# A four-layer graph network on one core: comparing adjacency counts four to a word, moving one PSUM tile and one matrix product, and one store to another queue

## The chip, the cores and the metric

The kernel runs on one core of a Trainium2 chip. The metric is the device time of a launch in microseconds, the median of the runs. A core has TensorE (PE) for matrix products and transposes, VectorE (DVE), ScalarE (ACT) and GpSimd (POOL) for the rest, and SyncE (SP), which here issues most of the DMA transfers; each of them works through its own queue of instructions, and they wait for one another by semaphores. The engines work on SBUF (128 partitions) and on PSUM, the banks that PE writes its products to.

## The reference, cut to what matters

A graph has 6250 nodes of 64 features and 206,250 directed edges: 100,000 edges in both directions, and a loop at every node. So the matrix A of edge counts between nodes is symmetric. Four layers follow one another, each on the normalised and clipped node features, each added to them:

```python
x = x + _L0_gnn_ref(h, ...)   # two graph convolutions: sums over the edges, with norm
x = x + _L1_gnn_ref(h, ...)   # one such sum
x = x + _L2_gnn_ref(h, edge_attr_64, src, dst, ...)
x = x + _L3_gnn_ref(edge_index, h)   # three such sums
```

The sums of layers L0, L1 and L3 are products of A (with norms) and the features. L2 alone uses the edges' own features:

```python
Vp = leaky_relu(V @ pAw + pAb) @ pBw + pBb
x = relu(E @ mlp_w1 + mlp_b1)
x = relu(x @ mlp_w2 + mlp_b2)
scale = sigmoid(x @ Bw + Bb)
shift = x @ Cw + Cb
msg = scale * Vp[src] + shift
M = clip(msg, EPS, None) ** 2
ssum = segment_sum(M, dst, n)          # and the root of its mean
```

## The kernel before

**Nodes and A.** The nodes make 49 blocks of 128 (`NB`), seven chunks (`NC`) of seven blocks (`CB`, 896 nodes, `W`). The first stage, up to about 535 us, counts the edges by products of one-hot matrices (PE L903, evicted by ACT L907) into a strip of half a chunk's columns, 14 strips (`CS`), and SP stores each finished strip to DRAM (L914) as FP8 counts in seven tensors `A[0]` to `A[6]`. The same stage computes the first convolution (PE L1042).

**Two sums, 535 to 1003 us.** `gather` (L1183) goes over A by 49 pieces of 896 x 896 counts (784 KB): SP loads a piece (L1187), PE makes 49 products with it (L1190), and 7 pieces make a chunk of sums. SP issues in the order of the program: the last strip's store, then the pieces.

**The edges, 1003 to 3654 us.** The edges come in 202 groups `G` of 1024 (8 to a partition, `J`). An order written out by hand for PE, ACT and DVE runs 208 slots (`slot`, L1588 on). Slot i works on several groups at once, in this order of code:

- `loaded(i+4)`: SP loads edge features `e` (L1500).
- `evicted` h2 of group i-3: ACT, from PSUM bank `p_2` (L1522).
- `biased`, `gated` of i-4: DVE adds the bias to the gates and shifts in `p_bc` (L1533), ACT takes the sigmoid (L1538).
- `read_them`: a comparison or an addition left from the slot before.
- `clipped` of i-4: DVE multiplies by the fetched `v` (L1543), adds the shift (L1544), clips (L1545).
- `fetched(i)`: POOL issues eight indirect gathers of `Vp` rows (L1506) into one of four buffers `v`; `turned_edges(i)`: PE transposes `e` (L1514); `layer` 1 of i-1 (L1518).
- half of the slot's work beside (see below).
- `squared`, `compared_nodes` of i-4: ACT squares the message twice (L1552 to bf16, L1553 to PSUM `p_m`, which is a buffer of the ring `p_sum`), DVE makes one-hot matrices `to` (L1558) and takes the rest that bf16 lost (L1612, L1624; ACT L1613).
- `added_to_nodes` of i-6 (DVE L1575 to L1583).
- `layer` 2 of i-2 into `p_2` (PE L1518), then `gates_and_shifts` of i-3 into `p_bc` (PE L1528); `p_bc` and `p_2` have one buffer each.
- evictions on ACT of `p_e` and `p_1`; the last part of the message on DVE (L1624).
- the other half of the work beside; `summed` of i-5 (PE L1566).

**Work beside.** The list `todo` is spread over the slots up to a chunk's end, n items a slot. It has three kinds of item:

- `here` loads a piece of A on SP.
- `crossed` is the check that A is symmetric. For 28 pairs of chunks (i, k) it turns a block of the piece on PE by products with the identity (L1412), three or four blocks to a PSUM tile of the ring `p_sum` (two buffers), and DVE compares it with the piece `there` from the other side of A (L1418), adding up the differences into one column of `unlike`. A pair has 14 such items, all 392. `there` is loaded on SP by one transfer a pair (L1405).
- `partial` is a part of L3's first sum: 21 products on PE (L750) into the ring `p_sum`, which DVE adds to `Y` (L1437).

The first four pairs of chunks are checked alone, in the first 35 or so slots; after that each chunk of nodes that is finished brings 56 comparisons, 14 sums and 7 loads over about 29 slots. At the end the differences are added up; if there are any, a general path computes everything without relying on the symmetry.

**The end, 3723 to 4127 us.** Two more passes of `gather` over A make the rest of L3.

Of the kernel before, what the change touches and what calls it, by code (L numbers as in the profile page):

```python
# [617 lines left out]
def fast(ctx, tc, bad, x, src, dst, edge_attr, W3, b3, W4, b4, w1, b1, w2, b2, Bw, Bb, Cw, Cb,  # L618
# [10 lines left out]
    def strip_of(s, bs):  # L629

        lo, hi = OF_CHUNK[s % 2]
        return A[s // 2][:, bs, lo * P:hi * P]
# [40 lines left out]
    def blocks(c):  # L673
        return slice(c * CB, (c + 1) * CB)
# [83 lines left out]
    def first_stage(ph):  # L758
# [136 lines left out]
        def placed(s, q, n, lo, hd):  # L895

            if q == 0:
                strips[s] = new_strip()
            for r in range(2 * n):
                p = psum.tile([P, SG, P], F32, name="p_a", bufs=2)  # L900
                for j in range(SG):
                    g = r * SG + j
                    nc.tensor.matmul(p[:, j, :2 * NB], lo[:, g // GQ, :, g % GQ],  # L903
                                     hd[:, g // GQ, :, g % GQ], start=True, stop=True)
                col = 2 * (q * 2 + r) * SG

                nc.scalar.activation(  # L907
                    strips[s][:, :, col:col + 2 * SG].rearrange("p b (j l) -> p b j l", l=2),
                    p[:, :, :2 * NB].rearrange("p j (b l) -> p b j l", l=2), AF.Copy,
                    saturate=False)  # L910
                if r % 2:
                    if q + n == portions(s) and r == 2 * n - 1:
                        lo_, hi_ = OF_CHUNK[s % 2]
                        nc.sync.dma_start(strip_of(s, slice(0, NB)),  # L914
                                          strips[s][:, :, :(hi_ - lo_) * P])
                    yield

        waiting = []
# [447 lines left out]
    with ExitStack() as ph:  # L1366
# [12 lines left out]
                 ((2, 6), (2, 3), (2, 4), (2, 2)), ((3, 6), (3, 4), (3, 5), (3, 0)),  # L1379
                 ((4, 6), (4, 5), (4, 0), (4, 1)), ((5, 6), (5, 0), (5, 1), (5, 2)))  # L1380
        FIRST = ((3, 3), (4, 4), (5, 5), (6, 6))
        unlike = cpool.tile([P, 28 * 2 * CB], F32, name="unlike")

        def order(pairs):
            ks = [k for _, k in pairs]
# [14 lines left out]
        def there(n):  # L1400

            if n < len(there_of):
                i, k = there_of[n]
                t = held["there", i, k] = mpool.tile([P, CB, W], COUNT, name="there", bufs=2)
                nc.sync.dma_start(t, A[i][:, blocks(k), :])  # L1405

        def crossed(n, i, k, b, a0, a1):
            if b == 0 and a0 == 0:
                there(there_of.index((i, k)) + 1)
            p = ps_a.tile([P, 4, P], F32, name="p_sum", bufs=2)  # L1410
            for a in range(a0, a1):
                nc.tensor.matmul(p[:, a - a0, :], held["here", i, k][:, a, b * P:(b + 1) * P], ident_b,  # L1412
                                 start=True, stop=True)
            of_there = held["there", i, k][:, b, a0 * P:a1 * P]

            def compared():
                junk = mpool.tile([P, 4 * P], BF16, name="junk", bufs=1)
                nc.vector.scalar_tensor_tensor(  # L1418
                    junk[:, :(a1 - a0) * P],
                    p[:, :a1 - a0, :].rearrange("p a q -> p (a q)"), 15.5, of_there, op0=OP.min,  # L1420
                    op1=OP.not_equal, accum_out=unlike[:, n:n + 1])

            return compared

# [18 lines left out]
        def plan(pairs, sums):  # L1443
            for at, (i, k) in enumerate(order(pairs) if sums else pairs):
                asked.append((i, k))
                todo.append((here, len(asked)))
                if at < len(pairs):
                    for b in range(CB):
                        for a0, a1 in ((0, 4), (4, CB)):
                            todo.append((crossed, len(crossings), i, k, b, a0, a1))  # L1450
                            crossings.append((i, k, b, a0))
                if sums:
                    todo.append((partial, i, 2 * k))
                    todo.append((partial, i, 2 * k + 1))
# [65 lines left out]
        def evicted(g, p, t, **how):  # L1520
            of[g][t] = mpool.tile([P, 512], F32, name=t)
            nc.scalar.activation(of[g][t], of[g].pop(p), **how)  # L1522
# [13 lines left out]
        def gated(g):  # L1536
            gate = of[g]["p_bc"][:, :, 0, :]
            nc.scalar.activation(gate, gate, AF.Sigmoid)  # L1538
# [8 lines left out]
        def squared(g):  # L1547
            m = of[g].pop("m")
            m3 = of[g]["m3"] = mpool.tile([P, J, 3, D], BF16, name="m3")
            p_m = of[g]["p_m"] = ps_a.tile([P, 512], F32, name="p_sum", bufs=2).rearrange(  # L1550
                "p (j f) -> p j f", f=D)
            nc.scalar.activation(m3[:, :, 0, :], m, AF.Square)  # L1552
            nc.scalar.activation(p_m, m, AF.Square)  # L1553
# [33 lines left out]
        def slot(i):  # L1587
            def at(later):  # L1588
                return 0 <= i - later < G

            if i + 4 < G:
                loaded(i + 4)
            if at(3):
                evicted(i - 3, "p_2", "h2", func=AF.Relu, bias=b2_c)
            if at(M_AT):
                biased(i - M_AT)
                gated(i - M_AT)
            read_them()
            if at(M_AT):
                clipped(i - M_AT)  # L1600
            if at(0):
                fetched(i)
                turned_edges(i)
            if at(1):
                layer(i - 1, w1_d, "eT", "p_1")
            n = -(-len(todo) // max(min(k for k in ends if k >= i) + 1 - i, 1))
            some_of(n - n // 2)
            if at(M_AT):
                squared(i - M_AT)
                compared_nodes(i - M_AT)  # L1610
                p_m, m3 = of[i - M_AT].pop("p_m"), of[i - M_AT]["m3"]
                nc.vector.tensor_sub(p_m, p_m, m3[:, :, 0, :])  # L1612
                nc.scalar.activation(m3[:, :, 1, :], p_m, AF.Copy)  # L1613
            done = added_to_nodes(i - ADD_AT) if at(ADD_AT) else []
            if at(2):
                layer(i - 2, w2_d, "h1", "p_2")
            if at(BC_AT):
                gates_and_shifts(i - BC_AT)
            if at(0):
                evicted(i, "p_e", "eT", func=AF.Copy)  # L1620
            if at(1):
                evicted(i - 1, "p_1", "h1", func=AF.Relu, bias=b1_c)
            if at(M_AT):
                nc.vector.tensor_sub(m3[:, :, 2, :], p_m, m3[:, :, 1, :])  # L1624
            read_them()
            some_of(n // 2)
            if at(SUM_AT):
                summed(i - SUM_AT)
            for c in done:
                finished(c)  # L1630

# [4 lines left out]
                slot(i)  # L1636
            read_them()

        assert not todo and len(crossings) == 28 * 2 * CB


        nc.vector.tensor_reduce(missed[:, 2:3], unlike, axis=AX.X, op=OP.add)
        ones_c = cpool.tile([P, P], F32, name="ones_c")
        nc.vector.memset(ones_c, 1.0)
        p_m = ps_a.tile([P, 512], F32, name="p_e")
# [98 lines left out]
```

## Time and profile before

| what | value |
|---|---|
| runs | 4137.59, 4135.94, 4144.2 us; median 4137.59 |
| the profiled execution | 4129.13 us, its span 4127.2 us |
| granted TensorE clock, mean | 0.848 |
| PE, DVE, ACT, POOL busy, share of the span | 71%, 56%, 30%, 39% |
| DMA | 388.84 MB, mean 94 GB/s |
| 510 to 550 us: PE busy | 29.8 of 40 us |
| 550 to 1003 us: PE busy | 430 of 453 us |
| 1040 to 3620 us: PE, DVE, ACT, POOL busy | 1587, 1541, 823, 1512 of 2580 us |
| 3730 to 4127 us: PE busy | 389 of 397 us |

The profile is of one execution. Each row of its groups names a line of the kernel, the engine, the operation and its operands (out<-in), then the count, the busy time in all with the mean of one in ns, and the idle time that the engine had just before these instructions, with what ended it. "issue" is time in which the engine waited for nothing that the profile shows; "remote" or "another core or an unknown queue" is a wait whose end the profile can't place, since this is one core. PEld is PE's loading of weights, which overlaps its products. A name with q behind it (SPq) is the engine's queue of instructions that are not counted as work, such as the issue of a DMA.

### The profile page before, as it was taken

What the parts mean: (1) busy time and instruction counts of PE and PEld (TensorE: products, weight loads), DVE (VectorE), ACT (ScalarE), POOL (GpSimd) and SP (SyncE); (2) the same over time, 40 slices, a digit from 0 to 9 for tenths busy, and PEclk for the clock granted to TensorE, in tenths of its full rate; (3) what the DMA queues carried; (4) which work ended last, traced back from release to release, by engine and by line L of the source; (5) the groups of instructions that cost most, each with busy time, mean ns of one, the idle gap of its engine ahead of it and who ended that gap; (6) DMA issues with size and microseconds to landing.
All of it is one profiled execution on the core that took longest, in us unless ns stands there. A gap on an engine that the chain in (4) does not pass through costs nothing.

```text
span 4127.2 us, 60291 instructions
## 1 busy us (share of the span) xinstructions
PE 2926.0 (71%) x23962; PEld 2233.0 (54%) x23962; DVE 2309.9 (56%) x5293; ACT 1240.5 (30%) x2061; POOL 1611.4 (39%) x1885
## 2 busy tenths in 40 slices
PE   1799989997455566666666666655666666679999
PEld 1788889996233333333433343333434343349999
DVE  5999935322555566655656565655655565662111
ACT  3677710001233333333333232333323333320000
POOL 5000010002556655555555565565555555510000
PEclk9899999998777777787877787777778787789999
DMA  3243375653222222222222222222222222126664
GB/s 114 58 111 87 96 222 188 200 185 118 57 57 58 58 56 57 58 78 54 75 54 63 72 58 71 61 57 57 79 56 63 63 65 63 44 98 190 202 205 157
DMA packets 229091, 388.84 MB, mean 94 GB/s; under 512 B 93482, under 2 KB 139482, under 8 KB 228543
## 3 DMA queue, kind: packets, MB, share of 16 engines
q1 hardware_dynamic: 170478, 322.28, 25.1%
q0 software_dynamic: 54816, 60.71, 7.3%
q8 instruction: 190, 3.11, 0.3%
q10 hardware_dynamic: 3504, 1.90, 0.2%
q14 instruction: 103, 0.84, 0.1%
HBM read 340.54 MB, written 44.21 MB: 93 GB/s over the span
## 4 chain that ended last, share of the span: by engine, by line
PE 38%; DVE 32%; another core or an unknown queue 15%; issue 7%; ACT 4%; DMA 2%; POOL 1%; DVEq 0%; ACTq 0%; SPq 0%; POOLq 0%
PE p_acc L1190 18%; DVE to L1558 5%; PE p_bc L1528 4%; PE p L1518 4%; PE p_sum L750 4%; DVE p_bc L1533 3%; DVE junk L1418 3%; DVE m L1543 3%; DVE hd L888 3%; DVE m L1544 3%; DVE lo L888 2%; DVE p_sum L1612 2%; PE p_s L1566 2%; ACT p_bc L1538 2%
## 5 line engine op out<-in xcount | busy, mean ns | idle before, releaser
L1506 POOL DMA_INDIRECT v<-Vp_dram,src_g x1616 | 1544.3, 956 | 1471.1 <-DVE m L1543 608.1
L1190 PE MATMUL p_acc<-U,piece 128*128 128x192 bf16 x9604 | 800.3, 246 | 11.5 <-DMA piece<-A 9.1
L1190 PEld LDWEIGHTS <-piece 128*128 128x128 fp8e4 x9604 | 795.4, 98 | 16.7 <-DMA piece<-A 9.3
L1528 PE MATMUL p_bc<-BC,h 128*128 128x256 f32 x1616 | 532.5, 480 | 310.6 <-DVE m L1544 265.1
L1528 PEld LDWEIGHTS p_bc<-BC,h 128*128 128x128 f32 x1616 | 379.8, 243 | 559.0 <-issue 424.7
L1412 PE MATMUL p_sum<-ident_b,piece 128*128 128x128 bf16 x1372 | 157.8, 248 | 501.5 <-issue 159.8
L1533 DVE TENSOR_TENSOR p_bc<-p_bc,bias 128x1024 f32<-128x1024 f32 x202 | 248.5, 1230 | 443.6 <-remote 355.3
L1412 PEld LDWEIGHTS <-piece 128*128 128x128 fp8e4 x1372 | 109.0, 110 | 694.8 <-issue 501.2
L1418 DVE SCALAR_TENSOR_TENSOR junk<-p_sum,there 128x512 bf16<-128x512 f32 (+1 forms) x392 | 242.1, 618 | 258.2 <-remote 142.5
L1518 PE MATMUL p<-h,w_d 128*128 128x512 f32 x404 | 276.2, 768 | 102.5 <-ACT h L1522 77.0
L1522 ACT ACTIVATE h<-p,b_c 128x512 f32<-128x512 f32 x404 | 264.3, 694 | 277.4 <-remote 143.5
L1201 DVE TENSOR_REDUCE zg<-p_acc 128x128 f32<-128x384 f32 x112 | 56.3, 507 | 514.4 <-PE p_acc L1190 513.9
L907 ACT ACTIVATE strip<-p_a 128x784 fp8e4<-128x784 f32 x392 | 301.5, 822 | 101.1 <-PE p_a L903 86.0
L750 PE MATMUL p_sum<-piece,U 128*64 128x448 fp8e4 x2058 | 259.9, 379 | 73.0 <-issue 33.3
L1558 DVE TENSOR_SCALAR to<-count,lane 128x128 bf16<-128x128 bf16 x1616 | 291.9, 264 | 0.0
L1552 ACT ACTIVATE m<-m 128x512 bf16<-128x512 f32 x202 | 127.6, 632 | 503.3 <-DVE m L1545 397.4
L1538 ACT ACTIVATE p_bc<-p_bc 128x512 f32<-128x512 f32 x202 | 117.6, 582 | 461.0 <-DVE p_bc L1533 387.5
L1518 PE MATMUL p<-eT,w_d 128*128 128x512 f32 x404 | 251.1, 708 | 5.2 <-issue 2.8
L750 PEld LDWEIGHTS <-U 128*64 128x64 bf16 x2058 | 126.5, 116 | 208.7 <-issue 119.8
L1566 PE MATMUL p_s<-m,to 128*128 128x192 bf16 x1616 | 215.9, 288 | 31.0 <-DVE H L1580 10.3
L1042 PE MATMUL p_sum<-U,strip 128*128 128x192 bf16 x2401 | 230.3, 248 | 0.0
L888 DVE TENSOR_TENSOR lo<-count,key 128x4096 bf16<-128x4096 bf16 (+1 forms) x103 | 225.1, 2185 | 0.0
(204 smaller groups left out, 3289.1 us busy)
## 6 DMA issues: line engine op xcount, KB each, us to landing
piece<-A SPq DMA_DIRECT2D x249, 784.0 KB
e<-in_edge_attr SPq DMA_DIRECT2D x202, 256.0 KB
v<-Vp_dram,src_g POOLq DMA_INDIRECT x1616
A<-strip SPq DMA_DIRECT2D x7, 3136.0 KB
there<-A SPq DMA_DIRECT2D x28, 784.0 KB
A<-strip SPq DMA_DIRECT2D x7, 2352.0 KB
pairs<-pair SPq DMA_DIRECT2D x1, 1616.0 KB
Vp_dram<-v SPq DMA_DIRECT2D x7, 224.0 KB
```

The costliest lines, as they stand in the source:

```text
L750: nc.tensor.matmul(p[half * D:(half + 1) * D, :w], U3[:, b, k, :], at_block, start=(i < 2), stop=(i >= 3 * n - 2))
L888: nc.vector.tensor_tensor(t, of.unsqueeze(1).to_broadcast(t.shape), key[:, k, at:at + n * 2 * SG].rearrange("p (h j) -> p h j", j=GQ) .uns ...
L907: nc.scalar.activation(strips[s][:, :, col:col + 2 * SG].rearrange("p b (j l) -> p b j l", l=2), p[:, :, :2 * NB].rearrange("p j (b l) -> ...
L1190: nc.tensor.matmul(p[d // 2][:, d % 2 * 3 * D:(d % 2 + 1) * 3 * D], t[:, b, d * P:(d + 1) * P], U3[:, k * CB + b, :, :].rearrange("p t f - ...
L1412: nc.tensor.matmul(p[:, a - a0, :], held["here", i, k][:, a, b * P:(b + 1) * P], ident_b, start=True, stop=True)
L1418: nc.vector.scalar_tensor_tensor(junk[:, :(a1 - a0) * P], p[:, :a1 - a0, :].rearrange("p a q -> p (a q)"), 15.5, of_there, op0=OP.min, op1 ...
L1506: nc.gpsimd.indirect_dma_start(out=v[:, j, :], out_offset=None, in_=Vp_dram[:, :], in_offset=bass.IndirectOffsetOnAxis(ap=src_g[:, g, j:j ...
L1518: nc.tensor.matmul(of[g][p], w, of[g].pop(x), start=True, stop=True)
L1528: nc.tensor.matmul(p_bc[:, 2 * q:2 * q + 2].rearrange("p j o f -> p (j o f)"), h2[:, q * P:(q + 1) * P], BC, start=True, stop=True)
L1533: nc.vector.tensor_tensor(p_bc, p_bc, bias.unsqueeze(1).to_broadcast([P, J, 2, D]), op=OP.add)
L1558: nc.vector.tensor_scalar(to[:, j, :], count, lane[:, g, j:j + 1], None, op0=OP.is_equal)
L1566: nc.tensor.matmul(p, to[:, j, :], m3[:, j].rearrange("p t f -> p (t f)"), start=(j == 0), stop=(j == J - 1))
```

## The change

Four things are edited.

1. The store of the last strip is issued on ACT's queue instead of SP's, and all strips are stored as pairs of counts (a bf16 view of the same bytes).
2. The check looks at counts as FP32 words of four. `there` has another layout: row 4x + j of a block lies in partition x (32 partitions to a block) at place j, so that four rows lie behind one another in a partition; a pair is loaded by seven transfers, one a block. `crossed` turns 128 or 96 word columns of three or four blocks by PE's FP32 transpose, which makes the four counts of a word four rows, and compares 2048 or 1536 counts at once, reading the PSUM tile as counts and `there` in steps of one row (896 bytes). A pair has 4 items instead of 14; all are 112 instead of 392.
3. `p_m`, the squared message in FP32, lies in the bank `p_2` instead of the ring `p_sum`.
4. `layer` 2 of group i-2 is made at the slot's end, behind `summed`, instead of ahead of the gates; h2's eviction on ACT comes behind `biased` and `gated` in the next slot instead of ahead of them.

```diff
@@ -911,8 +911,9 @@
                     if q + n == portions(s) and r == 2 * n - 1:
                         lo_, hi_ = OF_CHUNK[s % 2]
-                        nc.sync.dma_start(strip_of(s, slice(0, NB)),
-                                          strips[s][:, :, :(hi_ - lo_) * P])
+                        (nc.sync if s < CS - 1 else nc.scalar).dma_start(
+                            strip_of(s, slice(0, NB)).bitcast(BF16),
+                            strips[s][:, :, :(hi_ - lo_) * P].bitcast(BF16))
...
-        unlike = cpool.tile([P, 28 * 2 * CB], F32, name="unlike")
+        HALVES = ((0, 4), (4, CB))
+        unlike = cpool.tile([P, 28, 2, 2], F32, name="unlike")
+        nc.vector.memset(unlike, 0.0)
...
-                t = held["there", i, k] = mpool.tile([P, CB, W], COUNT, name="there", bufs=2)
-                nc.sync.dma_start(t, A[i][:, blocks(k), :])
-
-        def crossed(n, i, k, b, a0, a1):
-            if b == 0 and a0 == 0:
+                t = held["there", i, k] = mpool.tile([P, 2, 4, W], COUNT, name="there", bufs=2)
+                for d in range(CB):
+                    nc.sync.dma_start(
+                        t[d % 4 * 32:d % 4 * 32 + 32, d // 4],
+                        A[i][:, k * CB + d, :].rearrange("(x j) w -> x j w", j=4))
+
+        def crossed(n, i, k, h, a0, a1):
+            if h == 0 and a0 == 0:
                 there(there_of.index((i, k)) + 1)
+            x0, x1 = HALVES[h][0] * 32, HALVES[h][1] * 32
+            m = x1 - x0
             p = ps_a.tile([P, 4, P], F32, name="p_sum", bufs=2)
+            words = held["here", i, k].bitcast(F32)
             for a in range(a0, a1):
-                nc.tensor.matmul(p[:, a - a0, :], held["here", i, k][:, a, b * P:(b + 1) * P], ident_b,
-                                 start=True, stop=True)
-            of_there = held["there", i, k][:, b, a0 * P:a1 * P]
+                nc.tensor.transpose(p[:m, a - a0, :], words[:, a, x0:x1], ident)
+            of_there = held["there", i, k][:m, h, :, a0 * P:a1 * P]
 
             def compared():
-                junk = mpool.tile([P, 4 * P], BF16, name="junk", bufs=1)
+                junk = mpool.tile([P, 4, P, 4], BF16, name="junk", bufs=1)
                 nc.vector.scalar_tensor_tensor(
-                    junk[:, :(a1 - a0) * P],
-                    p[:, :a1 - a0, :].rearrange("p a q -> p (a q)"), 15.5, of_there, op0=OP.min,
-                    op1=OP.not_equal, accum_out=unlike[:, n:n + 1])
+                    junk[:m, :a1 - a0],
+                    p[:m, :a1 - a0, :].bitcast(COUNT).rearrange("p a (r j) -> p a r j", j=4),
+                    15.5, of_there.rearrange("p j (a r) -> p a r j", r=P), op0=OP.min,
+                    op1=OP.not_equal, accum_out=unlike[:m, n // 4, h, a0 // 4:a0 // 4 + 1])
...
-                    for b in range(CB):
-                        for a0, a1 in ((0, 4), (4, CB)):
-                            todo.append((crossed, len(crossings), i, k, b, a0, a1))
-                            crossings.append((i, k, b, a0))
+                    for h in range(2):
+                        for a0, a1 in HALVES:
+                            todo.append((crossed, len(crossings), i, k, h, a0, a1))
+                            crossings.append((i, k, h, a0))
...
-            p_m = of[g]["p_m"] = ps_a.tile([P, 512], F32, name="p_sum", bufs=2).rearrange(
+            p_m = of[g]["p_m"] = ps_a.tile([P, 512], F32, name="p_2").rearrange(
...
-            if at(3):
-                evicted(i - 3, "p_2", "h2", func=AF.Relu, bias=b2_c)
             if at(M_AT):
                 biased(i - M_AT)
                 gated(i - M_AT)
+            if at(3):
+                evicted(i - 3, "p_2", "h2", func=AF.Relu, bias=b2_c)
             read_them()
...
             done = added_to_nodes(i - ADD_AT) if at(ADD_AT) else []
-            if at(2):
-                layer(i - 2, w2_d, "h1", "p_2")
             if at(BC_AT):
                 gates_and_shifts(i - BC_AT)
...
                 summed(i - SUM_AT)
+            if at(2):
+                layer(i - 2, w2_d, "h1", "p_2")
```

The final addition over `unlike` follows its new shape.

More of the change, by code (lines that the diff above doesn't have):

```diff
@@ L1637, in fast @@
             read_them()
-        assert not todo and len(crossings) == 28 * 2 * CB
-        nc.vector.tensor_reduce(missed[:, 2:3], unlike, axis=AX.X, op=OP.add)
+        assert not todo and len(crossings) == 28 * 4
+        nc.vector.tensor_reduce(missed[:, 2:3], unlike.rearrange("p n h a -> p (n h a)"), axis=AX.X,
+                                op=OP.add)
         ones_c = cpool.tile([P, P], F32, name="ones_c")
```

## The prediction

> **What bounds the kernel now.** I read the page's span in slices first, then its groups, the table by windows, the chain of waits, and at two places the timeline. From 1040 to 3620 us the 202 edge groups run, 62% of the span, and no engine fills it. Columns of the window row: length, then PE, PEld, DVE, ACT and POOL busy (instructions), granted clock, DMA share, GB/s.
>
> ```profile
> 1040.00:3620.00 2580.00, 1587.42 (x7667) 980.16 (x7668) 1541.14 (x4234) 823.47 (x1421) 1511.71 (x1582) 0.78 0.24 61
> ```
>
> All three large engines are near 60%. So waits decide, and the page's groups say which:
>
> ```profile
> L1506 POOL DMA_INDIRECT v<-Vp_dram,src_g x1616 | 1544.3, 956 | 1471.1 <-DVE m L1543 608.1
> L1533 DVE TENSOR_TENSOR p_bc<-p_bc,bias 128x1024 f32<-128x1024 f32 x202 | 248.5, 1230 | 443.6 <-remote 355.3
> ```
>
> POOL's gathers wait for L1543 (which frees a `v`), and the bias waits for "remote", a release that the profile can't place. The timeline of one such stall (start, length, engine, operation; in brackets the idle time before and its end):
>
> ```profile
> 2096.91 0.95 POOL L1506 DMA_INDIRECT v<-Vp_dram,src_g  x1 [0.31 <-issue]
> 2100.60 1.23 DVE L1533 TENSOR_TENSOR p_bc<-p_bc,bias 128x1024 f32<-128x1024 f32 x1 [7.87 <-remote]
> 2101.74 0.68 DVE L1418 SCALAR_TENSOR_TENSOR junk<-p_sum,there 128x512 bf16<-128x512 f32 x1
> 2101.87 0.58 ACT L1538 ACTIVATE p_bc<-p_bc 128x512 f32<-128x512 f32 x1 [6.21 <-DVE p_bc L1533]
> ...
> 2102.48 0.69 DVE L1543 TENSOR_TENSOR m<-p_bc,v 128x512 f32<-128x512 f32 x1
> ...
> 2103.44 1.03 POOL L1506 DMA_INDIRECT v<-Vp_dram,src_g  x1 [5.59 <-DVE m L1543]
> ...
> 2108.08 1.23 DVE L1533 TENSOR_TENSOR p_bc<-p_bc,bias 128x1024 f32<-128x1024 f32 x1
> ```
>
> POOL ends 16 gathers at 2097.86 and has no free `v`. The bias resumes 2.74 us later, although PE had made its gates some 12 us before: PE's completions become visible late while gathers fly, and together once POOL pauses. I don't know why; I take it as a pattern. The chain of waits has this stall as its third part, by engine:
>
> ```profile
> PE 38%; DVE 32%; another core or an unknown queue 15%; issue 7%; ACT 4%; DMA 2%; POOL 1%; DVEq 0%; ACTq 0%; SPq 0%; POOLq 0%
> ```
>  The mul follows 1.88 us after the bias, the next gather 0.96 us after that, and the second slot of the pair (bias at 2108.08) meets no stall. Sixteen gathers 1.25 us apart take 15 x 1.25 + 0.95 = 19.7 us; with 2.7 + 1.9 + 1.0 that makes 25.3 us for two slots, 12.65 a slot. Pairs elsewhere take 25.3 to 25.4 whether they hold many comparisons or few, so engine work within a pair is mostly covered.
>
> 202 slots of 12.65 are 2555 us; the stage, counted from the 1040 to the last group's end at 3654, takes 2614. The 59 us above it sit where comparisons and partial sums come in bursts that break the pair: the stretch from 1429 to 1811 holds 29 slots in 382 us against 367.
>
> The other place is the border at 535 us:
>
> ```profile
> 534.48 0.51 SPq L914 DMA_DIRECT2D A<-strip  x1
> 535.10 14.00 SPq L1187 DMA_DIRECT2D piece<-A  x7
> ```
> ```profile
> 549.84 2.42 PE L1190 MATMUL p_acc<-U,piece 128*128 128x192 bf16 x14 [9.09 <-DMA piece<-A]
> ```
>
> SP issues the last strip, then the first piece; that one issue takes 9.3 us of the 14.0 (the next ones 1.2, 0.6 and 0.5), because the strip's descriptors are still in the same queue. PE waits 9.09 us.
>
> **The change, part by part.**
>
> 1. *Last strip on ACT's queue.* ACT has ended its strips, so nothing is queued behind the issue there for those microseconds; the piece leads on SP. The first piece needs only earlier strips (the fifth needs this one, landing some 11 us after 534.5). The Trainium skill ("Trainium Kernel Development and Optimization", Key Constraints) says that queues of different engines share the same 16 DMA engines and interleave, so another queue saves issue time alone. By that rule, if the wait were bandwidth, the gain is 0. The row says that 9.3 us were issue; the transfer itself still shares with the strip. I take the first product at about 541 to 542 in place of 549.84: **-8 us** (ends 0 and -10). PE is busy 430 of the next 453 us, so this passes on to the end. The bitcast to pairs leaves the bytes as they are: 0.
>
> 2. *Symmetry check by words, PE.* It removes 1372 products:
>
> ```profile
> L1412 PE MATMUL p_sum<-ident_b,piece 128*128 128x128 bf16 x1372 | 157.8, 248 | 501.5 <-issue 159.8
> L1418 DVE SCALAR_TENSOR_TENSOR junk<-p_sum,there 128x512 bf16<-128x512 f32 (+1 forms) x392 | 242.1, 618 | 258.2 <-remote 142.5
> ```
>
> It adds 392 FP32 transposes; the group L1514 has this form at 0.27 (median) to 0.32 us (mean): about 125 us. PE -33 us, and 980 instructions fewer. PE is off the path in a pair: 0 directly.
>
> 3. *The same, DVE.* By form, 512 elements take 684 ns and 384 take 551: 1.04 ns an element and 0.15 us fixed. So 2048 take 2.28 us and 1536 take 1.75. 56 of each are 226 us, with 84 ns for each accumulator read 235; before 242 + 33 = 275. DVE -40 us, hidden in pairs. But the new operand `there` is read in steps of 896 bytes. A rule speaks against it: the skill's "SBUF — State Buffer", on cachelines, has FP8 data fetched in lines of 16 bytes, each crossing paid. At a doubled cost the comparison takes 4.4 us and the check 470 us. The nearest row is L1244, 1024 elements in a 32-byte step, 1.086 us: 1.06 ns each, no penalty. I take the row (2.28), keep 4.4 for the range.
>
> 4. *Placement.* A chunk now has 37 items in 29 slots in place of 77: one or two a slot instead of three. Order of DVE by the built program: mostly bias, mul, `to`, sub, then one comparison or sum at the slot's end. About five slots of each chunk put a comparison between bias and mul. There the sigmoid, 0.58 us, covered the old one (0.68; mul starts 1.88 after the bias either way); a new one costs 2.28 - 0.68 = 1.6 us, where that slot is the stalled one. That is about half: 5 x 7 x 0.5 x 1.6 = **+28 us** at most, some of it in bursts that were broken anyway. In exchange, bursts of three comparisons and two sums go; the rest of the excess over 12.65 falls from about 14 us to about 5 a chunk. Net I put 8.5 for 14 over six chunks: **-33 us**. The first phase has 20 items in 35 slots instead of 60; some 12 slots are empty, at 12.3 in place of 12.65: **-4 us**. Ends for placement: +30 (bursts no shorter, mul late) and -130 (every slot like an empty one: 202 x 0.35 = 70, and the 59 us of excess gone).
>
> 5. *196 `there` DMAs instead of 28.* At 0.5 us of issue each (the row L914's) 84 us more of SP in 2600; behind them on SP are the `e` loads, four slots ahead (50 us), and pieces. The store of Vp on SP stands before most of them. 0; if the cover went, a late `e` would stall PE by some us a piece. Shorter rows (896 bytes x 4 a partition) move the same bytes at 24% DMA share.
>
> 6. *p_m in p_2's bank, layer2 at the slot's end, h2's eviction behind the gate.* No instruction more. p_sum's ring is left to checks and sums, which takes PE's waits for it away. New: layer2 waits for the sub L1624; the eviction (0.69 us) on ACT stands behind the sigmoid, which waits for the stalled bias; PE's gates wait for the eviction. In the stall the eviction would end about 2103.2, and the gates, bound by L1544 until 2104.04, start then anyway: cover 0.8 us. In the second slot gates can be late by 1 to 2 us, under the next stall of 8 us. 0; without cover +1 a pair, +100.
>
> **Sum.** -8 - 33 - 4 = -45 on the profiled execution: 4129.13 (span 4127.2, 2 around it) gives 4084. The median of the runs, 4137.59, lies 8.5 above, so I predict **about 4092 us**.
>
> **Rivals.** (a) *Only the border moves.* The pair is set by 16 gathers and the release, and excess returns as long comparisons: 4137.6 - 8 = 4129.5. For it: pairs indifferent to load. Against: the broken stretches. Chance 0.18, at the edge of no change. (b) *Slower: the long comparison enters POOL's way.* POOL runs on only if the second slot's mul comes within 10 us of the pair's first gather; its mul at 2109.96 is 3.5 us early. A comparison of 2.28 in place of 0.55 leaves 1.8; one of 4.4 none. Point: beyond about 4 us, or with two queued. Then 1.6 to 2.4 us on some 50 pairs, and up to 3.7 in the bias-to-mul slots (35 x 0.5 x 3.7 = 65): +80 to +185, less 45: **4172 to 4275**. For: the cacheline rule; against: L1244. Chance 0.22. (c) *The release comes sooner.* If PE's late completions are a matter of how many it has, 980 fewer let the bias come before POOL stops: 11.9 a slot, -150 and the border: **about 3980**. Empty slots at 12.3 speak for a little of it, not for much. Chance 0.14. (d) *It doesn't do what it says:* words altered on the way through PE would send the kernel to its general path, far slower; 0.02. My forecast: 0.44.
>
> The forecast alone is 4070 to 4115. Over all, 4010 to 4180. About 0.2% (8.3 us) is what can be told from no change. Faster: forecast 0.43, (c) 0.14, of (a) 0.06: 0.63. Same: of (a) 0.10, of (b) 0.02 and the rest: 0.14. Slower: 0.23.
>
> **What would show it.** First product at L1190 near 541, no 14.0 on SP there. The two comparison forms at 2.28 and 1.75 us (4.4 makes (b)). Pairs still 25.4 us; stretches of 29 slots near 375 instead of 380. Transposes near 0.3 us x392. PE's gates not waiting on ACT's eviction. Wrong if pairs change length at all, if the mul after L1506's pause comes over 2 us after the bias throughout, or if `e` is waited for.

## The result, and the profile after

The changed kernel takes 4186.06 us (median of 4 runs, 4170.85 to 4201.69), the kernel before 4140.9 beside it: ratio 1.012, interval 1.0102 to 1.0137. It is slower, by 45 us by the medians. The profiled execution after has a span of 4184.5 us, 57.3 more than before.

By stage: PE's first product of the two sums comes at 538.29 us (before 549.84), the last of these sums' products ends at 978.6 (984.8), the edges' first bias at 1030.0 (1039.8), and their last bias at 3709.4 (3651.3). From first bias to last are 2679.4 us for 2611.6. From PE's first product of the last two passes to the end of the span are 405.5 us in both. So the edge stage takes 68 us more, and this pair of executions reaches it 10 us earlier. How much of these 10 is the border's can't be read from one pair: in the nine profiles of this program and its variants in which the edge stage takes over 2600 us, the first bias lies anywhere between 1024 and 1046 us, on whichever queue the strip is stored.

The granted clock of PE in the stage is 0.77 for 0.78 before. By itself that is a small thing: one part in 77 of PE's 1472 busy us would be 19 us, if all of it stood in POOL's way (my estimate from these two figures).

The page's groups after, in the same columns as before, with the evictions' row of before ahead of them:

```profile
L1522 ACT ACTIVATE h<-p,b_c 128x512 f32<-128x512 f32 x404 | 264.3, 694 | 277.4 <-remote 143.5
```
```profile
L1515 POOL DMA_INDIRECT v<-Vp_dram,src_g x1616 | 1541.1, 954 | 1547.6 <-DVE m L1552 675.5
...
L1531 ACT ACTIVATE h<-p,b_c 128x512 f32<-128x512 f32 x404 | 277.6, 687 | 514.4 <-remote 446.8
L1426 DVE SCALAR_TENSOR_TENSOR junk<-p_sum,there 128x2048 bf16<-128x2048 fp8e4 (+1 forms) x112 | 361.0, 3224 | 70.1 <-remote 43.9
...
L1542 DVE TENSOR_TENSOR p_bc<-p_bc,bias 128x1024 f32<-128x1024 f32 x202 | 248.0, 1228 | 168.3 <-remote 91.8
```

"remote", which I read as the wait for PE's late completions, has moved: the bias had 355.3 us of it and has 91.8, the evictions on ACT had 143.5 and have 446.8. The comparison takes 3224 ns in the mean, where 2.0 us was forecast. POOL waits 67 us longer for the mul.

The view of waits, 1100 to 3600 us of the changed kernel (us in total, times, longest), says whom that holds up:

```profile
POOL v L1515 <- DVE m L1552: 632.8, 96, 16.5
...
ACT h L1531 <- remote: 425.4, 56, 18.2
...
PE p_bc L1537 <- ACT h L1531: 383.6, 45, 20.2
...
DVE p L1621 <- ACT p L1562: 261.7, 28, 16.6
```

PE's gates (L1537) wait for h2's eviction (L1531), and so does the middle of DVE's slot: the subtraction L1621 needs a square that stands behind the eviction in ACT's queue. Before, neither wait is among the large ones. One stop of POOL in the timeline of the changed kernel (start, length, engine, operation):

```profile
2381.43 0.94 POOL L1515 DMA_INDIRECT v<-Vp_dram,src_g  x1 [0.30 <-issue]
...
2385.69 0.69 ACT L1531 ACTIVATE h<-p,b_c 128x512 f32<-128x512 f32 x1 [14.08 <-remote]
...
2386.27 0.62 ACT L1561 ACTIVATE m<-m 128x512 bf16<-128x512 f32 x1
...
2386.79 0.59 ACT L1562 ACTIVATE p<-m 128x512 f32<-128x512 f32 x1
2387.42 0.70 DVE L1621 TENSOR_TENSOR p<-p,m 128x512 f32<-128x512 f32 x1 [12.52 <-ACT p L1562]
...
2388.81 0.68 DVE L1631 TENSOR_TENSOR m<-p,m 128x512 bf16<-128x512 f32 x1
...
2389.41 2.81 DVE L1426 SCALAR_TENSOR_TENSOR junk<-p_sum,there 96x1536 bf16<-96x1536 fp8e4 x1
...
2392.13 1.23 DVE L1542 TENSOR_TENSOR p_bc<-p_bc,bias 128x1024 f32<-128x1024 f32 x1
...
2393.40 0.58 ACT L1547 ACTIVATE p_bc<-p_bc 128x512 f32<-128x512 f32 x1 [3.59 <-DVE p_bc L1542]
...
2394.01 0.69 DVE L1552 TENSOR_TENSOR m<-p_bc,v 128x512 f32<-128x512 f32 x1 [0.65 <-ACT p_bc L1547]
...
2394.97 1.03 POOL L1515 DMA_INDIRECT v<-Vp_dram,src_g  x1 [12.60 <-DVE m L1552]
```

PE's layer2 for this eviction started at 2366.63 and took 1.05 us; ACT sees it at 2385.69, 18 us later and 3.3 after POOL's last gather. In the stop shown of before, the same release freed the bias, and the mul came 1.9 us on. Here the mul of that slot had run already (so POOL had its `v` and went on). The release frees the slot's rest: squares, subtractions, a comparison of 2.8 us, the next bias and sigmoid. The mul that POOL waits for comes 8.3 us after the release, and the stop is 12.6 us instead of 5.6.

Counted in the traces, over all stops of the gathers of more than 1.5 us:

| kernel | stops, us in all | stops over 8 us, us in all | stops that an eviction of ACT's (h2's, h1's or eT's) ends: number, mean us, of it after the release |
|---|---|---|---|
| before | 111, 616 | 6, 60 | 29, 5.96, 4.13 |
| after | 104, 686 | 30, 331 | 23, 9.70, 7.06 |

The last column puts a stop down to the instruction in it, on DVE or ACT, that had waited longest. The 70 us between the rows are the stage's 68. In 24 stops after a comparison starts, and they are 9.53 us long in the mean; the other 80 are 5.72 (before, with one comparison 5.51, with none 5.56).

### The profile page after: what moved, and what is told of

The parts are those of the page before. It is cut to its first block, busy times and chain, and to the rows that moved or that the text cites. A ratio compares the mean times of both kernels' runs of the same rounds, so it can differ in the third digit from the quotient of the medians.

```text
span 4184.5 us, 57689 instructions
## 1 busy us (share of the span) xinstructions
PE 2851.5 (68%) x22982; PEld 2186.3 (52%) x22982; DVE 2446.0 (58%) x4734; ACT 1233.4 (29%) x2061; POOL 1608.8 (38%) x1885
## 5 line engine op out<-in xcount | busy, mean ns | idle before, releaser
L1537 PE MATMUL p_bc<-BC,h 128*128 128x256 f32 x1616 | 576.1, 517 | 868.2 <-ACT h L1531 423.9
L1537 PEld LDWEIGHTS p_bc<-BC,h 128*128 128x128 f32 x1616 | 396.4, 257 | 1037.3 <-ACT h L1531 686.6
L1191 PEld LDWEIGHTS <-piece 128*128 128x128 fp8e4 x9604 | 795.3, 98 | 8.1 <-issue 7.7
L1531 ACT ACTIVATE h<-p,b_c 128x512 f32<-128x512 f32 x404 | 277.6, 687 | 514.4 <-remote 446.8
L1426 DVE SCALAR_TENSOR_TENSOR junk<-p_sum,there 128x2048 bf16<-128x2048 fp8e4 (+1 forms) x112 | 361.0, 3224 | 70.1 <-remote 43.9
L1621 DVE TENSOR_TENSOR p<-p,m 128x512 f32<-128x512 f32 x202 | 148.7, 736 | 342.9 <-ACT p L1562 273.5
L1542 DVE TENSOR_TENSOR p_bc<-p_bc,bias 128x1024 f32<-128x1024 f32 x202 | 248.0, 1228 | 168.3 <-remote 91.8
L1575 PEld LDWEIGHTS <-to 128*128 128x128 bf16 x1616 | 160.1, 112 | 195.3 <-issue 107.1
L1527 PE MATMUL p<-eT,w_d 128*128 128x512 f32 x404 | 236.9, 669 | 28.9 <-ACT h L1531 17.0
L1527 PE MATMUL p<-h,w_d 128*128 128x512 f32 x404 | 237.2, 666 | 13.8 <-issue 13.6
L1043 PE MATMUL p_sum<-U,strip 128*128 128x192 bf16 x2401 | 229.7, 247 | 0.0
L903 PE MATMUL p_a<-hd,lo 128*128 128x98 bf16 x3136 | 191.2, 214 | 29.0 <-DVE lo L888 22.0
```

The lines of the kernel that those rows point to most:

```text
L1043: nc.tensor.matmul(p[:, d * 3 * D:(d + 1) * 3 * D], strips[s][:, b, (d0 - lo + d) * P:(d0 - lo + d + 1) * P], U3[:, b, :, :].rearrange("p ...
L1191: nc.tensor.matmul(p[d // 2][:, d % 2 * 3 * D:(d % 2 + 1) * 3 * D], t[:, b, d * P:(d + 1) * P], U3[:, k * CB + b, :, :].rearrange("p t f - ...
L1426: nc.vector.scalar_tensor_tensor(junk[:m, :a1 - a0], p[:m, :a1 - a0, :].bitcast(COUNT).rearrange("p a (r j) -> p a r j", j=4), 15.5, of_th ...
L1527: nc.tensor.matmul(of[g][p], w, of[g].pop(x), start=True, stop=True)
L1537: nc.tensor.matmul(p_bc[:, 2 * q:2 * q + 2].rearrange("p j o f -> p (j o f)"), h2[:, q * P:(q + 1) * P], BC, start=True, stop=True)
L1542: nc.vector.tensor_tensor(p_bc, p_bc, bias.unsqueeze(1).to_broadcast([P, J, 2, D]), op=OP.add)
```

## The experiments

Two theories to begin with. **Long comparison:** 3.7 us where 0.7 stood delay the chain that frees `v`. **Order:** with layer2 at the slot's end and its eviction behind the gate, PE's late completion meets ACT, and what stands behind it. The first four kernels take the parts alone, and shorten the comparison in the whole. All four ran on one chip, on which the changed kernel itself was not run.

**Part 1 alone.** The first hunk of the change's diff (strips as pairs, the last one on ACT's queue), in the kernel before.

> The kernel before with part 1 alone (the last strip stored from ACT's queue, strips as pairs). In the profile of the changed kernel the first product of the two sums came 11.6 us earlier and the edges' first bias 9.8 us earlier. Both theories (order and long comparison) leave this part out of the loss, so -8 to -10 us against before: about 4131 from 4141. If the earlier start is eaten by the edge stage, 0.

4123.81 us against 4130.62 (ratio 0.9974, interval 0.9958 to 0.999): -7, as expected, though the interval reaches from -17 to -4.

**Part 2 alone.** The check by words in the kernel before; the rest undone from the changed kernel:

```diff
-                        (nc.sync if s < CS - 1 else nc.scalar).dma_start(
+                        nc.sync.dma_start(
...
-            p_m = of[g]["p_m"] = ps_a.tile([P, 512], F32, name="p_2").rearrange(
+            p_m = of[g]["p_m"] = ps_a.tile([P, 512], F32, name="p_sum", bufs=2).rearrange(
...
+            if at(3):
+                evicted(i - 3, "p_2", "h2", func=AF.Relu, bias=b2_c)
             if at(M_AT):
                 biased(i - M_AT)
                 gated(i - M_AT)
-            if at(3):
-                evicted(i - 3, "p_2", "h2", func=AF.Relu, bias=b2_c)
...
+            if at(2):
+                layer(i - 2, w2_d, "h1", "p_2")
             if at(BC_AT):
                 gates_and_shifts(i - BC_AT)
...
-            if at(2):
-                layer(i - 2, w2_d, "h1", "p_2")
```

> The kernel before with part 2 alone (the check by words; p_m in the ring p_sum, layer2 ahead of the gates, h2's eviction ahead of the bias, all strips on SP). Theory 'long comparison' (3.67 and 2.78 us on DVE in place of 0.68 and 0.55 delay the chain that frees v): the whole loss of the edge stage, +50 to +70 us. Theory 'order' (layer2 is seen late by ACT and the eviction of h2 holds up what is behind it): this part alone costs nothing, -30 to +10 us.

4131.22 against 4130.62 (1.0, 0.9987 to 1.0013). No loss: the long comparison by itself is not the cause. Nor is there the gain that the forecast put here.

**Parts 3 and 4 alone**, in the kernel before: the hunks of the change's diff for `p_m`, h2's eviction and layer2.

> The kernel before with parts 3 and 4 alone (p_m in p_2's bank, layer2 at the slot's end, h2's eviction behind the gate), check and strips as before. Theory 'order': ACT's eviction of h2 waits for over 400 us in all and the time is +50 to +80 us. Theory 'long comparison': no loss, -10 to +10 us.

4142.95 (1.0026, 1.0015 to 1.0036): +12. A loss, but a fifth of what the order theory expected; and the evictions wait 229.7 us for "remote" between 1100 and 3600 us, where it expected over 400.

**The changed kernel with short comparisons.** Each compares only the first 512 of its counts; three quarters or two thirds of the check are left out.

```diff
-                    junk[:m, :a1 - a0],
-                    p[:m, :a1 - a0, :].bitcast(COUNT).rearrange("p a (r j) -> p a r j", j=4),
-                    15.5, of_there.rearrange("p j (a r) -> p a r j", r=P), op0=OP.min,
+                    junk[:m, :1],
+                    p[:m, :1, :].bitcast(COUNT).rearrange("p a (r j) -> p a r j", j=4),
+                    15.5, of_there[:, :, :P].rearrange("p j (a r) -> p a r j", r=P), op0=OP.min,
```

> The changed kernel with each word comparison cut to its first 512 counts (the rest of the check is left out): about 0.98 us each in place of 3.67 and 2.78, transposes and transfers unchanged. Theory 'long comparison': the loss goes, 4120 to 4135 us. Theory 'order': DVE is freed by some 250 us and the time stays within 15 us of 4186.

The comparisons take 1.03 us, and the time is 4125.69 (0.998, 0.9967 to 0.9993): no loss against the kernel before. So neither theory holds alone. The parts add up to +5, the whole was +45 (beside another set of runs of the kernel before), and with a short comparison there is no loss though the order stays. A third theory: **the two work on each other**, the late eviction putting a comparison into POOL's stop as in the timeline above.

The waits of this kernel, in the same view as above, are those of the changed kernel all the same:

```profile
ACT h L1531 <- remote: 435.4, 50, 18.8
...
PE p_bc L1537 <- ACT h L1531: 335.2, 41, 20.9
...
DVE p L1621 <- ACT p L1562: 287.7, 31, 17.3
```

So the late eviction and what waits for it belong to the order, whatever the comparison's length. What differs is in the stops, here split by whether a comparison starts in them (one execution each; that of the last row was 22 us over its kernel's median, that of the first 17 under):

| kernel | stops, us in all | over 8 us, us in all | with a comparison: number, mean us, us in all | the others, us in all |
|---|---|---|---|---|
| words alone | 111, 615 | 19, 188 | 18, 8.80, 158 | 93, 456 |
| changed | 104, 686 | 30, 331 | 24, 9.53, 229 | 80, 457 |
| changed, short comparisons | 96, 644 | 24, 264 | 24, 6.44, 154 | 72, 490 |

Long comparisons lie in POOL's stops in the old order too (18 of them), and stops over 8 us are no sure sign of a loss. But between the first two rows the whole difference is in the stops with a comparison, and shortening the comparison takes it out of them again (while the others grow by 32 us).

The next four were to tell which two parts it is, and whether the place of the eviction or that of layer2. They ran on another chip, and the four after them on a third.

**The changed kernel again.**

> The changed kernel again, beside the next three on one chip. The parts measured alone gave -7 (strip), 0 (words) and +12 (order), which add up to +5; the whole was +45 to +57 on another chip. If the parts work on each other, +40 to +60 here too; if the loss belonged to that chip, +5.

3486.75 against 3497.06 (0.997, 0.9959 to 0.9981). Neither expected value: on this chip the kernel before is some 640 us shorter than on the first, and the change is faster by 10. The page of the changed kernel there:

```profile
L1515 POOL DMA_INDIRECT v<-Vp_dram,src_g x1616 | 1534.0, 949 | 885.2 <-issue 447.1
...
L1542 DVE TENSOR_TENSOR p_bc<-p_bc,bias 128x1024 f32<-128x1024 f32 x202 | 247.7, 1226 | 3.4 <-PE p_bc L1537 2.7
```

The bias waits 3.4 us in all, and nothing waits for "remote". POOL issues its 1616 gathers without one stop. From first bias to last are 2007.5 us for 201 slots, 9.99 each, which is eight gathers of 1.25 us. So on this chip POOL alone sets the edge stage, and what a change can gain lies ahead of it and behind it: I take the 10 us for the border's, though neither a run of the border alone nor a profile of the kernel before is on record for this kind of chip. Nearly all of the difference between the two chips lies in this stage (2679.4 us on the first): the first product of the two sums comes at 526.32 us for 538.29, and the last two passes take 405.4 for 405.5.

**The eviction ahead of the gate**, the rest as changed:

```diff
+            if at(3):
+                evicted(i - 3, "p_2", "h2", func=AF.Relu, bias=b2_c)
             if at(M_AT):
                 biased(i - M_AT)
                 gated(i - M_AT)
-            if at(3):
-                evicted(i - 3, "p_2", "h2", func=AF.Relu, bias=b2_c)
```

> The changed kernel with h2's eviction back ahead of the bias and the gate on ACT (layer2 still at the slot's end, p_m still in p_2's bank, check by words). Theory 'eviction behind the gate': a long comparison delays bias, then sigmoid, then the eviction, then PE's gates, so with the eviction first the loss goes: within 10 us of before. Theory 'layer2 at the end': the eviction is late because PE's last product of the slot is seen late, whatever stands ahead of it on ACT; now the sigmoid waits for it too: no better than the changed kernel, +40 or more.

3487.63 (0.9973, 0.9962 to 0.9983). It says nothing here, since there are no late completions.

**The comparison's loops exchanged**, the rest as changed:

```diff
-                junk = mpool.tile([P, 4, P, 4], BF16, name="junk", bufs=1)
+                junk = mpool.tile([P, 4, 4, P], BF16, name="junk", bufs=1)
...
-                    junk[:m, :a1 - a0],
-                    p[:m, :a1 - a0, :].bitcast(COUNT).rearrange("p a (r j) -> p a r j", j=4),
-                    15.5, of_there.rearrange("p j (a r) -> p a r j", r=P), op0=OP.min,
+                    junk[:m, :, :a1 - a0],
+                    p[:m, :a1 - a0, :].bitcast(COUNT).rearrange("p a (r j) -> p j a r", j=4),
+                    15.5, of_there.rearrange("p j (a r) -> p j a r", r=P), op0=OP.min,
```

> The changed kernel with the comparison's loops the other way round (place j outside, rows inside), so that the counts of there are read one after the other and those in PSUM in steps of 4 bytes; the same comparisons. If the step of 896 bytes is what made them 3.66 and 2.79 us, they take about 2.3 and 1.75 us now, DVE is freed by about 130 us, and the time falls to between 4125 and 4150; if it is the reading of FP8 in PSUM or the three loops, they stay at 3.66 or get longer, and the time stays at +45.

The groups by form, of the changed kernel on this chip and then of this one:

```profile
L1426 DVE SCALAR_TENSOR_TENSOR junk<-p_sum,there 128x2048 bf16<-128x2048 fp8e4 x27 | 99.3, 3676 | 0.0
...
L1426 DVE SCALAR_TENSOR_TENSOR junk<-p_sum,there 128x1536 bf16<-128x1536 fp8e4 x27 | 75.4, 2792 | 0.0
```
```profile
L1426 DVE SCALAR_TENSOR_TENSOR junk<-p_sum,there 128x2048 bf16<-128x2048 fp8e4 x27 | 61.6, 2280 | 0.0
...
L1426 DVE SCALAR_TENSOR_TENSOR junk<-p_sum,there 128x1536 bf16<-128x1536 fp8e4 x27 | 47.2, 1747 | 0.0
```

2280 and 1747 ns are the forecast's 2.28 and 1.75. The order in which the operands are walked costs (3676 - 2792) / 512 = 1.73 ns a count for (2280 - 1747) / 512 = 1.04. The time, 3489.95 (0.9979), is no better than the changed kernel's here: 136 us less of DVE are off the path.

**Parts 3 and 4 undone**, parts 1 and 2 left: the diff shown for part 2 without its first hunk.

> The changed kernel with parts 3 and 4 undone (strip on ACT and check by words stay). If the long comparison and the new order work on each other, this is -8 us against before (the strip's gain, words 0). If the long comparison works on the earlier start instead, +30 or more.

3488.96 (0.9976, 0.9966 to 0.9985): the same gain.

**The same four again**, on a third chip, where before takes 3495.13.

> The changed kernel once more. On the chip of the last four runs before itself took 3497 us in place of 4131 to 4141 and POOL's gathers never stopped; there the change gained 10 us. If this chip is of the first kind (before near 4130), the loss comes back, +40 to +60; if of the other, -10 again.

> The changed kernel with h2's eviction ahead of the bias and gate again, on this chip. On a chip of the first kind: theory 'eviction behind the gate' expects it within 10 us of before; theory 'layer2 at the end is seen late' expects +40 or more. On one of the other kind -10 by both.

> The changed kernel with the comparison's place j as its outer loop, which made it 2.28 and 1.75 us in place of 3.67 and 2.79. On a chip of the first kind: if the length of the comparison is what the new order does not bear, +0 to +20 us against before (the cut comparison of about 1.0 us gave -5); if lengths over some 2 us already do the harm, +40.

> The changed kernel with parts 3 and 4 undone. On a chip of the first kind: if the long comparison and the new order work on each other, about -8 us (strip -7, words 0); if the long comparison and the earlier start do, +30 or more. On one of the other kind -8.

In this order: 3486.28, 3487.89, 3488.38, 3487.94 us, ratios 0.9973 to 0.9981. The second chip's numbers again.

**Three of them once more**, now on a chip where before takes 4164.52:

> The changed kernel, in search of a chip on which before takes about 4130 us. There: +40 to +60 if the parts work on each other (alone they added up to +5); about +5 if the first chip was a case by itself. On a chip where before takes about 3496: -10.

> The changed kernel with parts 3 and 4 undone. Where before takes about 4130: -8 if it is the long comparison and the new order that work on each other; +30 or more if it is the long comparison and the earlier start. Where before takes about 3496: -8.

> The changed kernel with h2's eviction ahead of the bias and gate. Where before takes about 4130: within 10 us of before if the eviction's place behind the gate does the harm; +40 or more if it is layer2's place at the end of PE's slot. Where before takes about 3496: -8.

| kernel | us | ratio to before | interval | POOL's stops | stops over 8 us | with a comparison: number, mean us, us in all |
|---|---|---|---|---|---|---|
| changed | 4213.80 | 1.0133 | 1.0106 to 1.016 | 109, 697 us | 27, 301 us | 22, 10.22, 225 |
| eviction ahead of the gate | 4154.29 | 0.9972 | 0.9962 to 0.9982 | 109, 654 us | 10, 124 us | 13, 7.78, 101 |
| parts 3 and 4 undone | 4144.55 | 0.9955 | 0.9943 to 0.9967 | 111, 651 us | 23, 242 us | 20, 9.06, 181 |

The loss is there again, on a chip of the first kind, and two lines of the slot's code take it away: with the eviction ahead of the gate 59.5 of the 69 us between the first row and the last are back. The words stay, layer2 stays at the slot's end, `p_m` stays in the bank `p_2`. So it is the eviction's place behind the gate that makes the loss, with the long comparison there. Against parts 3 and 4 undone the stops with a comparison again hold nearly all that the changed kernel's stops have more (44 of 46 us), and with the eviction ahead fewer comparisons start in a stop. In the view of waits of the kernel with the eviction ahead PE's gates no longer wait for it:

```profile
PEld p_bc L1537 <- issue: 830.0, 186, 16.7
ACT h L1531 <- remote: 697.9, 81, 10.7
PE p_bc L1537 <- DVE m L1553: 642.6, 117, 15.2
POOL v L1515 <- DVE m L1552: 629.1, 112, 16.6
```

The eviction waits for "remote" longer than ever, 697.9 us. But it now stands at the head of the slot, so that the sigmoid and the mul follow at once. A stop from its timeline:

```profile
2334.53 2.74 DVE L1426 SCALAR_TENSOR_TENSOR junk<-p_sum,there 128x1536 bf16<-128x1536 fp8e4 x1 [2.74 <-PE p L1527]
...
2336.39 0.95 POOL L1515 DMA_INDIRECT v<-Vp_dram,src_g  x1 [0.30 <-issue]
...
2340.23 1.23 DVE L1542 TENSOR_TENSOR p_bc<-p_bc,bias 128x1024 f32<-128x1024 f32 x1 [2.94 <-remote]
2340.36 0.69 ACT L1531 ACTIVATE h<-p,b_c 128x512 f32<-128x512 f32 x1 [8.23 <-remote]
...
2342.11 0.69 DVE L1552 TENSOR_TENSOR m<-p_bc,v 128x512 f32<-128x512 f32 x1 [0.65 <-ACT p_bc L1547]
...
2343.07 1.03 POOL L1515 DMA_INDIRECT v<-Vp_dram,src_g  x1 [5.73 <-DVE m L1552]
```

The comparison of this stop runs ahead of the release, in time in which DVE would wait anyway; bias and eviction are freed together, and the mul is 1.9 us behind. In the counts, the stops that an eviction ends are 72 here with 5.49 us each, 2.76 of it after the release; in the changed kernel on this chip 23 with 10.41 and 7.77.

**The last three** were to say whether the eviction's place is enough without layer2's, and whether the loss follows the comparison's length.

> Strip on ACT, check by words, and of the new order only h2's eviction behind the bias and gate (layer2 ahead of the gates and p_m in the ring, as before). Where before takes 4130 us or more: if the eviction's place together with the long comparison is enough, +40 to +60 us against before; if it also needs layer2 at the slot's end, whose product is then seen last, -20 to 0 as with parts 3 and 4 undone. Where before takes about 3496: -8.

> The changed kernel with the comparison at 2.28 and 1.75 us in place of 3.67 and 2.79 (place j as the outer loop). Where before takes 4130 us or more: -5 to +15 if the loss follows the comparison's length (1.0 us gave -5 and 3.67 gave +50); +40 if any comparison over 2 us does it. Where before takes about 3496: -7.

> Strip on ACT and check by words with the shorter comparison, in the old order: a version to beat both. Where before takes 4130 us or more: -20 (as with the long comparison, which this order hides) to -30. Where before takes about 3496: -8.

The first has the part-2 diff without the strip's and the eviction's hunks, the second the exchanged loops, the third these in the old order with the strip on ACT. Before took 3495.22 on the chip that they ran on, and they took 3489.28, 3489.11 and 3488.65 (each 0.9982, 0.9975 to 0.9989). On this chip nothing waits for PE's completions either, so both questions stay open for the chips with the loss. Of the length, only the ends were tried there, 1.0 and 3.7 us.

The version to take is the strip on ACT with the check by words in the old order: it beats the kernel before on both kinds of chip (0.9955 and 0.9976 to 0.998) and the changed kernel by 69 us where that loses.

## Why the prediction was wrong, step by step

The forecast was -45 us; +45 came. Two of its terms failed: the placement (3), which was to bring 37 of the 45, brought nothing, and the new order (4), put at 0, turned the sign.

1. *The border, -8.* Right in kind and, as far as the interval of the -7 alone can say, in size: the issue time was what moved. But "nothing is queued behind the issue there" was wrong. On ACT's queue, the columns being start, length, engine:

```profile
532.18 0.61 ACTq L914 DMA_DIRECT2D A<-strip  x1
532.83 15.84 ACTq L665 DMA_DIRECT2D pAw_d<-in_L_gnn_pAw  x1
548.71 1.25 ACTq L665 DMA_DIRECT2D pBw_d<-in_L_gnn_pBw  x2
550.06 0.60 ACT L1085 ACTIVATE feat<-p_node 128x512 f32<-128x512 f32 x1 [17.91 <-issue]
```

   The issue of a weight's load behind the strip takes 15.84 us, where with the strip on SP it took 0.61 (at 533.80 in the trace of before). The eviction behind it starts at 550.06, and PE waits 3.74 us for that in place of 9.09 for the piece. Of 11.6 us at the first product 6.2 are left when PE ends the two sums.
2. *Comparison 2.28 and 1.75 us.* Mis-sized: 3.66 and 2.79. I chose the row L1244 (4-byte numbers in a 32-byte step, no penalty) over the rule of the Trainium skill ("SBUF — State Buffer", the note on cachelines), which spoke against the change. The rule names a penalty but no size; the 4.4 us were my doubling, and the measured value lies between 2.28 and that. (At 4.4 the check's sum would have been some 444 us, not the 470 that I wrote, since the fixed parts don't double.) The row was too unlike: one operand of 4-byte integers in SBUF says little of one-byte counts stepped by 896 bytes against PSUM. That the order of the loops makes the difference was shown (2.28 and 1.75 with them exchanged); which of the two operands pays was not.
3. *Placement, -33 and -4.* Failed. With words alone the time is as before (ratio 1.0): POOL's stops come to 615 us for 616, since the 18 with a comparison in them are 8.80 us and the 93 others 4.91. What the others are shorter than before's 5.5, those with a comparison are longer, in sum.
4. *The new order, 0, "cover 0.8 us".* **This is the step that failed and turned the sign.** I had asked whether the eviction would be late behind the sigmoid and found it covered, taking the sigmoid's wait for the only one. But the eviction has a wait of its own, for layer2, whose completion is seen as late as the gates' was. Behind the gate it became the place where the release arrives, 425.4 us of it. I had named what stands behind it, PE's gates, and overlooked the squares on ACT and with them the rest of DVE's slot. In place of a cover of 0.8 us, 7.06 us (4.13 before) passed from an eviction of ACT's to the end of the stops that it ends. Putting the eviction back ahead of the gate, and nothing else, gave back 59.5 us on the second chip with the loss. The comparison's length has its part in it: with short ones in the same order there was no loss. "+1 a pair, +100" was the price that I named for a missing cover; the stage took 68.
5. *Rival (b)*, the long comparison in POOL's way, gave 4172 to 4275 (4277 by its own sum) and holds 4186, but not as told, and so in part by luck. Its point, "beyond about 4 us, or with two queued" in a pair's second slot, is not where it happened: 3.7 us with the old order cost nothing. With the new order it did, and the stops with a comparison hold what came on top; that a release at the eviction leaves the comparison ahead of POOL's mul is shown in one stop, and not counted over all.
6. *Pairs of 25.3 us indifferent to load*: held for the old order, and there in the sum only (3). With the new order and long comparisons it failed.
7. *The rest* held: the transposes take 0.30 us each, and in the profile after no wait in the edge stage is put down to `e` or `there`. Of rival (c), a release that comes sooner, nothing shows: the release comes 2.6 us after POOL pauses in the kernel before and 2.7 in the changed one (medians over the stops).

## What to carry to other kernels

When a completion is seen late, by whatever cause, ask at which instruction the release arrives, and count the work from there to what the bounding engine waits for; moving a waiting instruction one place down its queue can put a whole slot into that path. Parts that cost 0 and 12 us alone cost some 50 together, as far as runs on different chips can be set side by side; so the whole has to be measured, and on more than one chip. A queue from which a large store is taken becomes free, and on the one that it is given to the next issue, and the compute behind it, waits.

## What the runs showed of the hardware

- **Chips of two kinds.** The kernel before takes 4130 to 4165 us in three sets of runs (on at least two chips) and 3495 to 3497 in three others, on three different chips; in the traces of the variants there POOL's gathers never stop once the stage runs. On the former the waits that I read as waits for PE's products end a while after POOL's gathers pause: the first one put down to "remote" in each stop ends 2.6 us after the pause in the kernel before and 2.7 in the changed one (medians), in the stop shown 18 us after the product. That it is the chip and not the kernel is what the same two kernels on both kinds show. The cause wasn't found. The granted clock in the edge stage differs too, 0.77 and 0.78 for 0.87, while from 550 to 960 us it is 0.99 and 1.00; these runs don't tell whether it is cause or effect. The eleven runs of variants on the second kind lie between 3486 and 3490 us.
- **One-byte counts on DVE** took 1.73 ns each when neighbours in the inner loop lay 896 bytes apart in SBUF, and 1.04 ns with the loops exchanged, where the other operand, in PSUM, is read in steps of 4 bytes (from the rows shown above).
- **An issue behind a strip's store** of 2352 KB in the same queue took 9.3 us on SP and 15.8 us on ACT; the same load's issue on ACT, with no strip ahead of it, took 0.61 us.
